# A graph attention kernel: the two gathers of a step of layer 1 stand apart, with the matmul stages rearranged around them

## The chip, the cores and the metric

The kernel runs on one core of a Trainium2 chip. A core has five engines with an instruction stream each: TensorE (PE in the profile; its weight loads are PEld), VectorE (DVE), ScalarE (ACT), GpSimd (POOL) and SyncE (SP). They run side by side and wait for each other by semaphores only. DMA engines move data between DRAM and the core's memory; a DMA is issued by an instruction of some engine. The metric is the time of one execution on the device in microseconds (us), as the median of several runs.

## The reference: what is computed

```python
B, N, C = x.shape            # 8, 2048, 64
H, D, _ = Wh.shape           # 4, 64
mask = graph + jnp.eye(N, dtype=graph.dtype) > 0
h = jnp.einsum('bnc,hdc->bhnd', x, Wh)
out_h = _gat_layer(h, mask[None, None], bh[None, :, None, :])
cat = jnp.transpose(out_h, (0, 2, 1, 3)).reshape(B, N, H * D)
z = jax.nn.leaky_relu(cat, negative_slope=0.2)
h2 = jnp.einsum('bnk,dk->bnd', z, Wo)
out2 = _gat_layer(h2, mask[None], bo)
z2 = jax.nn.leaky_relu(out2, negative_slope=0.2)
mu = jnp.mean(z2, axis=-1, keepdims=True)
var = jnp.mean(jnp.square(z2 - mu), axis=-1, keepdims=True)
out = (z2 - mu) * jax.lax.rsqrt(var + LN_EPS) * gamma + beta
...
x = _layernorm(x + out, axis=-1)
```

`_gat_layer(h, mask, b)` takes scores h times h transposed, keeps those where the mask is set, applies softmax over the neighbours and sums the neighbours' h with these weights, plus b. So there are two layers of attention over a graph: the first with four heads per batch element, the second with one. The adjacency is sparse. Node 0 has the most neighbours, and the number falls with the node's index.

## The kernel before

The first 56 nodes ("hubs") have so many neighbours that they are treated densely, in a prologue. The other 1992 nodes are cut into 166 sets of 12. For a set, the kernel finds the union of its nodes' neighbours, at most 128 of them, and gathers their rows from a table in DRAM: row m holds the values of node m for all 8 batch elements, with columns of ones for the softmax sums. From these 128 rows the scores of the 12 nodes are computed as small dense blocks, with a mask.

Layer 1 runs in 83 groups of two sets. Its loop (L1110, `for i in range(-4, NG + 3)`) is a software pipeline written out by hand: a step i works on several groups, each at another stage. The order in which the stages are written is the order of the instructions on each engine, since every engine works through its stream in order. The framework adds the semaphore waits where one engine's result is another's input, or where a buffer is still in use. In step i, in the order before, stand:

- scores of group i + 1 (L826, 64 small matmuls) and weigh (L831, DVE: scores minus mask, out of the tensor memory);
- project of group i - 1 (L532, 16 matmuls with the head weights) and leaky (L519, ACT: bias);
- two ACT copies xTg (L1129) of the gathered rows that the step before transposed into bank 0 and bank 1;
- lift (L838, ACT: exp), values of group i (L851, 32 matmuls: weights times gathered rows), and invert (L858 reciprocal and L859 multiplication on DVE, which gives osb);
- the two gathers of group i + 5 (L797 on POOL, an indirect DMA each). Their buffers come from a ring of ten, so they wait until values of group i have read theirs;
- own_rows (L805, POOL: copies the sets' own columns of x, for four sets, in every second step), and from step 30 load_own (SP: loads of xb) and add_beta (L933, POOL: adds beta to a piece of x that layer 2 uses) in alternate steps;
- leak (L524, DVE: the leaky ReLU of z);
- side jobs: the rest of the hubs' layer 1 (`hub_later`: turn_back, through_heads, to_table, for two halves, in steps 0 to 5), adjacency loads, and the building of the neighbour lists of the sets of later groups (`make_keys`, `pick`);
- second_maps of group i - 2 (L885, 8 matmuls with Wo), second_rows of group i - 3 (L895, one transpose), columns of group i + 4 (L811, 4 matmuls: the sets' own rows times the Gram matrices of the heads);
- keep_own (L890 on DVE, then L891 on POOL), keep_rows (L899 on DVE, then L902, writes to layer 2's table by SP), keep_columns (L817, ACT);
- turn bank 0 (L513, 4 transposes of gathered rows), turn_values (L868, 4 transposes of osb) with keep_values (L875, two ACT copies), turn bank 1 (L513).

The tensor memory holds one buffer for each of the tags S (scores), C (`cat`: project, second_maps, second_rows and columns of a step share it by slices) and O (values and turned values), and the two banks. Layer 2 begins after the loop. In the names of the rows `g` is a tile of gathered rows, `y` the kept columns, `e` the weights, `o` the values, `own` and `rowt` the results on their way to layer 2.

Of the kernel before, what the change touches and what calls it, by code (L numbers as in the profile page):

```python
# [359 lines left out]
def fast_kernel(ctx: ExitStack, tc: tile.TileContext, x, adj, Wh, bh, Wo, bo, gamma, beta, out, flag):  # L360
# [262 lines left out]
    def hub_later(t, new):  # L623
# [13 lines left out]
        def through_heads():  # L637
            cat = new(f"cath{t}", "C")
            project(held.pop(("oth", t)), cat, n)
            z = held["zh", t] = leaky(cat, n, f"zh{t}")  # L640
            leak(z)
# [158 lines left out]
    def own_rows(m):  # L800

        w = min(4, NS - 4 * m)
        t = held["x", m] = work.tile([P, 2 * GM], F32, tag="xo", name=f"xo{m}", bufs=2)
        src = xT[:, :, HUB:].rearrange("c q (k s) -> c s q k", s=NS)[:, 4 * m:4 * m + w]
        nc.gpsimd.tensor_copy(t[:, :w * 48].rearrange("c (s q k) -> c s q k", s=w, q=Q), src)  # L805
# [195 lines left out]
    own_rows(0)  # L1001
    own_rows(1)
# [107 lines left out]
    for i in range(-4, NG + 3):  # L1110
# [4 lines left out]
        if i >= 1 and slow and len(slow) % 3:  # L1115
            slow.pop(0)()
        cat = one(f"cat{i}", "C") if i <= NG else None
        if i < NG:
            ph, pr = cat[:, 0, 384:384 + GM], cat[:GM, 1, 384:512]
        else:  # L1120
            cat = one(f"cat{i}", "S" if i == NG + 1 else "C")
            ph, pr = cat[:, 0, :GM], cat[:GM, 1, :P]
        if 0 <= i - 1 < NG:
            project(held.pop(("ot", i - 1)), cat, GM)
            held["z", i - 1] = leaky(cat, GM, f"z{i - 1}")
        if 0 <= i + 2 < NG:
            t = held["T", 1, i + 2] = work.tile([P, 2, 512], F32, tag="xTg", name=f"xTg{i + 2}", bufs=3)
            for k in range(2):
                nc.scalar.copy(t[:, k, :], bank[k])  # L1129
        if 0 <= i + 1 < NG:  # L1130
            lift(i + 1)
        if 0 <= i < NG:
            op = one(f"o{i}", "O")
            values(i, op)
            invert(i, op)
        if 0 <= i + LOOK < NG and i > -3:
            for j in range(2):
                gather(table1, 2 * (i + LOOK) + j, 1, rows_tile)
        if NG - LOOK <= i < NG - 1:
            for j in range(2):  # L1140
                k = 2 * (i - NG + LOOK) + j
                hub_block(k, rows_tile(f"gh{k}"))
        if i + 6 < NG and i % 2 == 0 and i >= -2:
            own_rows((i + 6) // 2)
        if i >= 60 and i % 2 == 0 and ahead_of_second:
            ahead_of_second.pop(0)()
        if 0 <= (i - 30) // 2 <= NV:
            (add_beta if i % 2 else load_own)((i - 30) // 2)
        if 0 <= i - 1 < NG:
# [325 lines left out]
```

## Time and profile before

| | us |
|---|---|
| time, median of 3 runs | 1018.35 |
| the runs | 1017.01, 1018.35, 1022.75 |
| profiled execution: span | 1021.0 |

The busy time of the engines in the whole span, its course in 40 slices, and the costliest groups that concern the loop of layer 1:

```profile
PE 807.8 (79%) x18437; PEld 685.5 (67%) x18437; DVE 617.2 (60%) x1376; ACT 521.4 (51%) x1042; POOL 481.3 (47%) x614
...
PE   3976679899999999999999998419786676667760
...
PEclk9989989999999999999999999658999999999985
```

```profile
L797 POOL DMA_INDIRECT g<-table,index x166 | 176.6, 1064 | 207.2 <-PE o L851 165.7
...
L826 PE MATMUL s<-y,xTg 64*64 64x48 f32 x5312 | 115.4, 222 | 5.4 <-issue 3.5
...
L851 PE MATMUL o<-g,e 128*64 128x65 f32 x2656 | 98.0, 226 | 2.4 <-issue 2.4
...
L811 PE MATMUL cat<-xo,gram 128*128 128x192 f32 (+1 forms) x320 | 65.0, 326 | 0.0
```

In the first block the share of the span stands in brackets and the number of instructions behind the x. A digit of the slices is the busy share in tenths (9 is 90% or more), one slice being 1021.0 / 40 = 25.5 us; PEclk is the granted clock of TensorE in tenths. Slices 7 to 24, about 157 to 620 us, are the loop of layer 1. In the second block a row is a group of instructions by line, engine and operands: number, busy time in us and mean of one in ns, then the idle time of the engine just before them and what ended most of it; "issue" is time in which the engine waited for nothing that the profile shows. Matmuls overlap, so that the mean of one is longer than the distance from one to the next. In rows of the timeline, further down, consecutive instructions of one kind are one row: start, length from the first one's start to the last one's end, number, and in brackets the idle time before it with what ended it.

### The profile page before, as it was taken

To read this page: it belongs to the slowest core of one execution; us is meant where nothing else is said; L and a number is where in the kernel's file an instruction comes from. 1 tells how busy PE (TensorE), PEld (TensorE's weight loads), DVE (VectorE), ACT (ScalarE), POOL (GpSimd) and SP (SyncE) were. 2 spreads that over 40 slices of the span, in tenths; PEclk is the share of its full clock that TensorE was granted. 3 is DMA by queue.
4 is the path that set the end of the run, shared out by engine and by line. 5 is a ranking of instruction groups with operands and counts; after the bars stand their busy time and mean duration, and the time that the engine had idled before them with its cause. 6 is when DMAs were issued, how large, how long until landed. Compare 5 with 4: busy or idle time off the path is not lost.

```text
span 1021.0 us, 42671 instructions
## 1 busy us (share of the span) xinstructions
PE 807.8 (79%) x18437; PEld 685.5 (67%) x18437; DVE 617.2 (60%) x1376; ACT 521.4 (51%) x1042; POOL 481.3 (47%) x614
## 2 busy tenths in 40 slices
PE   3976679899999999999999998419786676667760
PEld 2644457788898888888888887307665555555750
DVE  3449844678777777745555555002267766766795
ACT  2423335556566666666666665005445645555651
POOL 6533214474454555556556630750456556655100
PEclk9989989999999999999999999658999999999985
DMA  8876412453233344444444432764345555445221
GB/s 184 238 208 171 118 44 59 131 134 80 75 91 83 103 124 123 120 124 115 120 119 113 120 86 75 193 184 128 91 112 141 152 147 142 125 134 138 76 53 29
DMA packets 81790, 122.52 MB, mean 120 GB/s; under 512 B 35568, under 2 KB 51852, under 8 KB 81594
## 3 DMA queue, kind: packets, MB, share of 16 engines
q0 software_dynamic: 26784, 65.84, 24.9%
q1 hardware_dynamic: 37702, 49.57, 16.3%
q10 hardware_dynamic: 17108, 4.30, 2.3%
q8 instruction: 147, 2.41, 1.0%
q14 instruction: 49, 0.40, 0.1%
HBM read 123.91 MB, written 18.48 MB: 139 GB/s over the span
## 4 chain that ended last, share of the span: by engine, by line
PE 56%; DVE 13%; issue 9%; ACT 8%; another core or an unknown queue 6%; DMA 4%; POOL 2%; SPq 1%; DVEq 0%; POOLq 0%; ACTq 0%
PE s L826 10%; PE o L851 8%; PE bank L513 7%; PE t L513 6%; PE cat L811 5%; ACT xts L1368 3%; DMA raw<-in_adj_dram 3%; PE cat L532 3%; PE o L868 3%; PE cat L885 3%; PE bank L1234 2%; PE bank L1223 2%; PE cat L895 2%; PE o L1253 2%
## 5 line engine op out<-in xcount | busy, mean ns | idle before, releaser
L797 POOL DMA_INDIRECT g<-table,index x166 | 176.6, 1064 | 207.2 <-PE o L851 165.7
L797 POOL DMA_INDIRECT rows<-table,index x166 | 170.0, 1024 | 147.3 <-PE o L1253 87.5
L831 DVE TENSOR_TENSOR e<-s,mask 128x768 f32<-128x768 f32 x83 | 79.4, 957 | 95.2 <-PE s L826 94.8
L826 PE MATMUL s<-y,xTg 64*64 64x48 f32 x5312 | 115.4, 222 | 5.4 <-issue 3.5
L513 PE MATMUL t<-ident,rows 128*128 128x128 f32 x664 | 91.6, 280 | 31.8 <-issue 30.4
L826 PEld LDWEIGHTS s<-y,xTg 64*64 64x64 f32 x5312 | 98.9, 134 | 25.6 <-issue 20.2
L1368 ACT COPY xts<-t 128x1024 f32<-128x1024 f32 x83 | 79.9, 1011 | 56.2 <-PE t L513 48.5
L513 PEld LDWEIGHTS t<-ident,rows 128*128 128x128 f32 x664 | 76.3, 144 | 40.9 <-issue 39.8
L513 PE MATMUL bank<-ident,g 128*128 128x128 f32 x664 | 100.2, 274 | 0.2 <-ACT otbh L634 0.2
L851 PE MATMUL o<-g,e 128*64 128x65 f32 x2656 | 98.0, 226 | 2.4 <-issue 2.4
L519 ACT ACTIVATE z<-cat,bhp 128x192 f32<-128x192 f32 x166 | 60.7, 417 | 73.9 <-PE cat L532 70.8
L851 PEld LDWEIGHTS o<-g,e 128*64 128x64 f32 x2656 | 85.8, 138 | 12.8 <-issue 3.0
L1129 ACT COPY xTg<-bank 128x512 f32<-128x512 f32 x166 | 89.1, 596 | 0.5 <-PE bank L513 0.3
L1223 PE MATMUL bank<-xts,share 128*32 128x128 f32 x1328 | 56.2, 278 | 34.4 <-issue 19.7
L513 PEld LDWEIGHTS bank<-ident,g 128*128 128x128 f32 x664 | 79.9, 142 | 2.8 <-DVE keysi L766 0.6
L838 ACT ACTIVATE e<-e,shifts 128x768 f32<-128x768 f32 x83 | 80.0, 964 | 2.5 <-DVE e L831 2.5
L817 ACT COPY y<-cat 128x384 f32<-128x384 f32 (+1 forms) x80 | 40.7, 509 | 68.5 <-DVE rowt L899 37.3
L598 ACT ACTIVATE e<-e,shifts 128x896 f32<-128x896 f32 x32 | 33.4, 1043 | 81.4 <-DVE e L595 65.6
L1223 PEld LDWEIGHTS bank<-xts,share 128*32 128x32 f32 x1328 | 38.1, 109 | 50.9 <-issue 44.2
L681 POOL TENSOR_SCALAR a<-raw 120x1024 bf16<-120x1024 int32 (+1 forms) x34 | 38.5, 1135 | 62.1 <-DMA raw<-in_adj_dram 34.7
L811 PE MATMUL cat<-xo,gram 128*128 128x192 f32 (+1 forms) x320 | 65.0, 326 | 0.0
L858 DVE RECIPROCAL rall<-o 64x8 f32<-64x8 f32 x166 | 34.1, 205 | 50.5 <-PE o L851 49.1
(190 smaller groups left out, 1563.0 us busy)
## 6 DMA issues: line engine op xcount, KB each, us to landing
raw<-in_adj_dram SPq DMA_DIRECT2D x32, 480.0 KB
table<-xb SPq DMA_DIRECT2D x22, 256.0 KB
xr_s<-table SPq DMA_DIRECT2D x21, 256.0 KB
table<-x SPq DMA_DIRECT2D x16, 260.0 KB
x<-in_x_dram ACTq DMA_DIRECT2D x32, 128.0 KB
table<-rowt SPq DMA_DIRECT2D x164, 24.4 KB
xb<-in_x_dram SPq DMA_DIRECT2D x164, 24.0 KB
out_dram<-y_s SPq DMA_DIRECT2D x162, 24.0 KB
```

Source lines behind the costliest of these rows:

```text
L513: nc.tensor.transpose(tp[:, q * P:(q + 1) * P], rows[:, q, 1:1 + P], ident)
L519: nc.scalar.activation(z[:, hp], cat[:, :, hp * n:(hp + 1) * n], AF.Identity, bias=bhp[:, hp:hp + 1], scale=1.0)
L797: nc.gpsimd.indirect_dma_start(out=t.rearrange("n q c -> n (q c)"), out_offset=None, in_=table, in_offset=bass.IndirectOffsetOnAxis(ap=ind ...
L811: nc.tensor.matmul(cat[:, k, 2 * GM:2 * GM + n], gram[:, g % 2 * 2 + k, :], held["x", g // 2][:, :n], start=True, stop=True)
L817: nc.scalar.copy(held["y", g // 2][:, :n, g % 2 * 2:g % 2 * 2 + 2], cat[:, :, 2 * GM:2 * GM + n].rearrange("p a n -> p n a"))
L826: nc.tensor.matmul(sp[half(r), p, (q * 2 + j) * M:(q * 2 + j + 1) * M], xt[half(p), j, q, half(r)], y[half(p), (j * Q + q) * M:(j * Q + q ...
L831: nc.vector.tensor_tensor(e[:, :16 * M].rearrange("p (a q n) -> p a q n", a=2, q=Q), sp[:, :, :8 * M].rearrange("p a (q n) -> p a q n", q= ...
L838: nc.scalar.activation(e[:, :16 * M], e[:, :16 * M], AF.Exp, bias=shifts[:, 0:1], scale=1.0)
L851: nc.tensor.matmul(op[half(p), j, o0:o0 + K1], e[:, c0:c0 + 64], rw[j][:, q, sums(p)], start=True, stop=True)
L1129: nc.scalar.copy(t[:, k, :], bank[k])
L1223: nc.tensor.matmul(sp[q * 32:(q + 1) * 32, k, :], bd[u % 3][:, k, q, :], xt[:, s % 2, q, :], start=True, stop=True, tile_position=(0, q * 32))
L1368: nc.scalar.copy(t, tp)
```

## The change

The step's stages get a new order. On PE: scores, project, columns, second_rows, side jobs, values, second_maps, both turns (bank 0 and bank 1), turn_values. On ACT the xTg copies stand before leaky, and keep_columns comes before values. On DVE keep_rows follows weigh, and keep_own still follows leak. On POOL the first gather stands right behind values, then the copy of keep_own, then own_rows, now for two sets in every step and no longer for four in every second one, and then the second gather; add_beta comes last. The hubs' jobs are all called at one place, one a step from step 0, and the projected hub values use tag S for their buffer in the tensor memory, not C. `cat` is allocated in the same way in every step.

```diff
--- before.py
+++ after.py
@@ -635,7 +635,7 @@
                            pt.rearrange("c (w n) -> c w n", w=8)[:, :, :HV].rearrange("c w (n h) -> c h w n", h=H))
 
         def through_heads():
-            cat = new(f"cath{t}", "C")
+            cat = new(f"cath{t}", "S")
             project(held.pop(("oth", t)), cat, n)
             z = held["zh", t] = leaky(cat, n, f"zh{t}")
             leak(z)
@@ -797,12 +797,16 @@
         nc.gpsimd.indirect_dma_start(out=t.rearrange("n q c -> n (q c)"), out_offset=None, in_=table,
                                      in_offset=bass.IndirectOffsetOnAxis(ap=index[:, s:s + 1], axis=0), **bound)
 
-    def own_rows(m):
-
-        w = min(4, NS - 4 * m)
-        t = held["x", m] = work.tile([P, 2 * GM], F32, tag="xo", name=f"xo{m}", bufs=2)
-        src = xT[:, :, HUB:].rearrange("c q (k s) -> c s q k", s=NS)[:, 4 * m:4 * m + w]
-        nc.gpsimd.tensor_copy(t[:, :w * 48].rearrange("c (s q k) -> c s q k", s=w, q=Q), src)
+    def own_rows(m, j):
+
+        w = min(2, NS - 4 * m - 2 * j)
+        if j == 0:
+            held["x", m] = work.tile([P, 2 * GM], F32, tag="xo", name=f"xo{m}", bufs=2)
+        if w <= 0:
+            return
+        s0 = 4 * m + 2 * j
+        src = xT[:, :, HUB:].rearrange("c q (k s) -> c s q k", s=NS)[:, s0:s0 + w]
+        nc.gpsimd.tensor_copy(held["x", m][:, j * 96:j * 96 + w * 48].rearrange("c (s q k) -> c s q k", s=w, q=Q), src)
 
     def columns(g, cat):
 
@@ -998,8 +1002,9 @@
     for g in range(LOOK - 2):
         for j in range(2):
             gather(table1, 2 * g + j, 1, rows_tile)
-    own_rows(0)
-    own_rows(1)
+    for m in range(2):
+        for j in range(2):
+            own_rows(m, j)
     for t in range(2):
         hub_end(t)
     for e in es:
@@ -1112,46 +1117,29 @@
             sp = one(f"s{i + 1}", "S")
             scores(i + 1, sp)
             weigh(i + 1, sp)
-        if i >= 1 and slow and len(slow) % 3:
-            slow.pop(0)()
-        cat = one(f"cat{i}", "C") if i <= NG else None
-        if i < NG:
-            ph, pr = cat[:, 0, 384:384 + GM], cat[:GM, 1, 384:512]
-        else:
-            cat = one(f"cat{i}", "S" if i == NG + 1 else "C")
-            ph, pr = cat[:, 0, :GM], cat[:GM, 1, :P]
+        cat = one(f"cat{i}", "S" if i == NG + 1 else "C")
+        ph, pr = cat[:, 0, 384:384 + GM], cat[:GM, 1, 384:512]
         if 0 <= i - 1 < NG:
             project(held.pop(("ot", i - 1)), cat, GM)
-            held["z", i - 1] = leaky(cat, GM, f"z{i - 1}")
         if 0 <= i + 2 < NG:
             t = held["T", 1, i + 2] = work.tile([P, 2, 512], F32, tag="xTg", name=f"xTg{i + 2}", bufs=3)
             for k in range(2):
                 nc.scalar.copy(t[:, k, :], bank[k])
+        if 0 <= i - 1 < NG:
+            held["z", i - 1] = leaky(cat, GM, f"z{i - 1}")
+        if 0 <= i + 4 < NG + NG % 2:
+            columns(i + 4, cat)
+        if 0 <= i - 3 < NG:
+            second_rows(i - 3, pr)
+            keep_rows(i - 3, pr)
         if 0 <= i + 1 < NG:
             lift(i + 1)
-        if 0 <= i < NG:
-            op = one(f"o{i}", "O")
-            values(i, op)
-            invert(i, op)
-        if 0 <= i + LOOK < NG and i > -3:
-            for j in range(2):
-                gather(table1, 2 * (i + LOOK) + j, 1, rows_tile)
-        if NG - LOOK <= i < NG - 1:
-            for j in range(2):
-                k = 2 * (i - NG + LOOK) + j
-                hub_block(k, rows_tile(f"gh{k}"))
-        if i + 6 < NG and i % 2 == 0 and i >= -2:
-            own_rows((i + 6) // 2)
-        if i >= 60 and i % 2 == 0 and ahead_of_second:
-            ahead_of_second.pop(0)()
-        if 0 <= (i - 30) // 2 <= NV:
-            (add_beta if i % 2 else load_own)((i - 30) // 2)
-        if 0 <= i - 1 < NG:
-            leak(held["z", i - 1])
+        if 0 <= i + 4 < NG + NG % 2:
+            keep_columns(i + 4, cat)
         if i >= 0:
             if turns():
                 some(1)
-            if slow and len(slow) % 3 == 0:
+            if slow:
                 slow.pop(0)()
             more(1)
             if todo3 and i == todo3[0][0]:
@@ -1162,29 +1150,39 @@
                 picks = pick(2)
                 done = NS
             assert i + 1 + LOOK >= NG or 2 * (i + 1 + LOOK) + 1 < ready
-
+        if 0 <= i < NG:
+            op = one(f"o{i}", "O")
+            values(i, op)
+            invert(i, op)
+        if 0 <= i - 1 < NG:
+            leak(held["z", i - 1])
+        if 0 <= i + LOOK < NG and i > -3:
+            gather(table1, 2 * (i + LOOK), 1, rows_tile)
+        if NG - LOOK <= i < NG - 1:
+            for j in range(2):
+                k = 2 * (i - NG + LOOK) + j
+                hub_block(k, rows_tile(f"gh{k}"))
         if 0 <= i - 2 < NG:
             second_maps(i - 2, ph)
-        if 0 <= i - 3 < NG:
-            second_rows(i - 3, pr)
-        if 0 <= i + 4 < NG + NG % 2:
-            columns(i + 4, cat)
+        if 0 <= i + 3 < NG:
+            for j in range(2):
+                turn(bank[j], rows[1, 2 * (i + 3) + j])
+        if 0 <= i < NG:
+            turn_values(i, op)
+            keep_values(i, op)
         if 0 <= i - 2 < NG:
             keep_own(i - 2, ph)
-        if 0 <= i - 3 < NG:
-            keep_rows(i - 3, pr)
+        if i >= -2 and 2 * ((i + 6) // 2) < NG:
+            own_rows((i + 6) // 2, i % 2)
+        if 0 <= i + LOOK < NG and i > -3:
+            gather(table1, 2 * (i + LOOK) + 1, 1, rows_tile)
+        if i >= 60 and i % 2 == 0 and ahead_of_second:
+            ahead_of_second.pop(0)()
+        if 0 <= (i - 30) // 2 <= NV:
+            (add_beta if i % 2 else load_own)((i - 30) // 2)
         for _ in range((2 if i < 22 or i % 2 else 1) if i >= 0 else 0):
             if not turns():
                 some(1)
-        if 0 <= i + 4 < NG + NG % 2:
-            keep_columns(i + 4, cat)
-        if 0 <= i + 3 < NG:
-            turn(bank[0], rows[1, 2 * (i + 3)])
-        if 0 <= i < NG:
-            turn_values(i, op)
-            keep_values(i, op)
-        if 0 <= i + 3 < NG:
-            turn(bank[1], rows[1, 2 * (i + 3) + 1])
         if NG - 3 <= i < NG:
             hub_step(i - NG + 3, bank[0])
     for k in range(3, 9):
```

## The prediction

> **What bounds the kernel now.** I read the windows view first, over the loop of layer 1 (columns: length, busy time with instruction count of PE, PEld, DVE, ACT and POOL, granted clock, DMA share, GB/s), cut at the starts of the scores stage of steps 6, 24, 31, 78 and 79.
>
> ```profile
> 210.22:313.10 102.88, 99.41 (x2488) 87.71 (x2487) 85.66 (x224) 63.26 (x145) 52.15 (x71) 1.00 0.35 90
> 351.19:609.85 258.66, 252.41 (x6441) 226.02 (x6440) 160.88 (x401) 168.29 (x381) 150.18 (x186) 1.00 0.43 117
> 609.85:614.66 4.81, 4.81 (x139) 4.35 (x138) 2.89 (x7) 3.31 (x9) 0.27 (x1) 1.00 0.30 71
> ```
>
> From step 6 on PE is busy 97% of the time at full granted clock; DVE and ACT have a third free and POOL 40% and more. So PE's order sets the pace. The first two windows hold 18 and 47 steps: 5.72 and 5.50 us each. The last row is a step in which no gather of this loop is issued any more: 4.81 us. Its PE rows in the timeline (start, length, work):
>
> ```profile
> 609.85 1.15 PE L826 MATMUL s<-y,xTg 64*64 64x48 f32 x64
> 610.82 0.53 PE L532 MATMUL cat<-otb,whT 64*64 64x96 f32 x16
> 611.28 1.15 PE L851 MATMUL o<-g,e 128*64 128x65 f32 x32
> 612.26 0.50 PE L885 MATMUL cat<-z,woT 128*64 128x96 f32 x8
> 612.69 0.32 PE L895 MATMUL cat<-ident,own 128*96 128x128 f32 x1
> 612.85 0.58 PE L811 MATMUL cat<-xo,gram 128*128 128x96 f32 x4
> 613.26 0.60 PE L513 MATMUL bank<-ident,g 128*128 128x128 f32 x4
> ```
>
> From start to start: scores 0.97, project 0.46, values 0.98, second_maps 0.43, second_rows 0.16, columns 0.41. Columns are half as wide here; full ones take 0.65 (403.80 to 404.45 below), a turn 0.44 (404.45 to 404.89). So 4.81 + 0.24 = 5.05 us is a step of PE alone, and 0.4 to 0.45 us of a 5.50 step is something else. An ordinary step, first its PE rows, then those of DVE, POOL and ACT:
>
> ```profile
> 403.22 0.50 PE L885 MATMUL cat<-z,woT 128*64 128x96 f32 x8
> 403.65 0.31 PE L895 MATMUL cat<-ident,own 128*96 128x128 f32 x1
> 403.80 0.82 PE L811 MATMUL cat<-xo,gram 128*128 128x192 f32 x4
> 404.45 0.60 PE L513 MATMUL bank<-ident,g 128*128 128x128 f32 x4
> 404.89 0.55 PE L868 MATMUL o<-ident,osb 112*128 112x112 f32 x4
> 405.27 0.60 PE L513 MATMUL bank<-ident,g 128*128 128x128 f32 x4
> 405.81 0.56 PE L826 MATMUL s<-y,xTg 64*64 64x48 f32 x24
> 406.62 0.87 PE L826 MATMUL s<-y,xTg 64*64 64x48 f32 x40 [0.25 <-issue]
> ```
>
> ```profile
> 403.43 0.42 DVE L858 RECIPROCAL rall<-o 64x8 f32<-64x8 f32 x2 [0.53 <-PE o L851]
> 403.89 0.69 DVE L859 TENSOR_TENSOR osb<-o,rall 128x512 f32<-128x512 f32 x1
> 404.50 0.55 DVE L524 SCALAR_TENSOR_TENSOR z<-z 128x384 f32<-128x384 f32 x1
> 405.22 0.26 DVE L890 COPY own<-cat 128x96 f32<-128x96 f32 x1 [0.17 <-PE cat L811]
> ```
>
> ```profile
> 403.56 1.02 POOL L797 DMA_INDIRECT g<-table,index  x1 [2.25 <-PE o L851]
> 404.88 1.05 POOL L797 DMA_INDIRECT g<-table,index  x1 [0.31 <-DMA table<-rowt]
> 405.95 1.27 POOL L933 TENSOR_TENSOR xb<-xb,bet 128x512 f32<-128x512 f32 x1
> ```
>
> ```profile
> 406.73 0.54 ACT L875 COPY otb<-o 128x192 f32<-128x192 f32 x2 [0.44 <-PE o L868]
> ```
>
> After the second gather has begun (404.88) PE starts 4 + 4 + 24 = 32 matmuls and then stands still inside the scores, put down to "issue", until 406.62: 0.69 us after that gather's end at 405.93. ACT's copy L875 gets the signal of a transpose whose row ended at 405.44 only at 406.73. I read it so: while a gather's instruction runs on POOL, and about half a microsecond longer, PE's completions can come late, and PE can run only some 32 matmuls ahead. Slow matmuls (columns, turns: 0.10 to 0.16 us each) spend that allowance slowly, so the first gather costs nothing; fast ones (scores 0.015, project and values 0.03) spend it at once. Over 29 steps the waits view gives
>
> ```profile
> PEld s L826 <- issue: 9.0, 43, 0.5
> ...
> PE s L826 <- issue: 1.9, 9, 0.4
> ```
>
> which is 10.9 / 29 = 0.37 us a step. That is what the change can win or multiply.
>
> **The change, part by part.** Counts of matmuls, ACT and DVE work stay; own_rows (L805) is cut in halves. Let X be the moment at which the values' last signal arrives (403.41 above) and s the start of the next scores.
>
> *First gather.* It still starts at X + 0.15 and lies over second_maps, eight turns and L868, all slow or few: 20 matmuls, no loss.
>
> *L868.* The turns ahead of it are now second_maps and both L513 stages: 0.43 + 0.44 + 0.44, from X - 0.19, so PE is at L868 at X + 1.12. Its input osb ends with L859 at 404.58 = X + 1.17. So PE waits about 0.1 us that it did not wait, taken as 0.13 with the signal; the bounds are 0 (before, the four columns and a turn covered it) and 0.69, the length of L859, if DVE comes to it so late. Then s = X + 1.77.
>
> *Second gather.* On POOL it now stands behind keep_own's copy L891, which waits for DVE's L890, and behind half of own_rows. DVE runs L858, L859, L524 to 405.05 (X + 1.64), then L890 0.26; the POOL costs are
>
> ```profile
> L891 POOL COPY own<-own 128x96 f32<-128x96 f32 x59 | 16.1, 273 | 14.4 <-DVE own L890 14.3
> L805 POOL COPY xo<-xT 128x192 f32<-128x192 f32 (+1 forms) x28 | 14.4, 515 | 0.2
> ```
>
> and a gather starts 0.15 after what it waited for (403.56 after X). So 1.64 + 0.26 + 0.27 + 0.26 + 0.15 = X + 2.58, that is s + 0.8. It ends at s + 1.85, and the stretch with late completions at about s + 2.35. In that stretch PE now has: 10 scores left, 16 of project, 4 columns, 1 second_rows = 31 matmuls, which last until s + 0.97 + 0.46 + 0.65 + 0.16 = s + 2.24. With an allowance of 32 the loss is 0.1 us instead of 0.37.
>
> *What waits on it.* add_beta (L933, 1.27 us) now follows the second gather: X + 2.58 + 1.03 + 1.27 = X + 4.9, ahead of the next first gather at X + 5.3. The rows of a gather are used five groups later. SP's writes from keep_rows come earlier and nothing waits for them. On DVE keep_rows now stands between weigh and invert: if the scores' signal too comes only at s + 2.35, weigh (0.96) and keep_rows (0.28) end at s + 3.6, and the values' signal is there at s + 5.25 - 1.77 = s + 3.5: L859, and with it L868, up to 0.15 later. I charge half of that in the 47 steps from 31 on, in most of which xb is loaded, and nothing before.
>
> *Steps 0 to 5.* The hub jobs run here. PE waited
>
> ```profile
> PE hh L650 <- DVE e L831: 2.1, 2, 1.1
> PE cat L532 <- ACT zh L519: 1.8, 2, 0.9
> ```
>
> 3.9 us in all. The jobs now come behind columns and second_rows, when weigh is nearly done, and through_heads no longer takes the tile that project needs. I take all 3.9; the bounds are 0 (the waits return at L851) and twice the sum, 8.
>
> The span of the profiled execution is on the page:
>
> ```profile
> span 1021.0 us, 42671 instructions
> ```
>
> *Sum.* Per step -0.37 + 0.13 + 0.10 = -0.14 in the 25 steps 6 to 30, so -3.5; -0.14 + 0.07 in 47 steps, so -3.3; hub -3.9: together -10.7. The profiled span, 1021.0, lies 2.65 above the median 1018.35 and inside the runs shown (1017.01 to 1022.75); off the median the sum is 1007.6, and I say **1007**. Below: all of the 0.45 goes, on 72 steps, with 0.13 for L868: -23, and hub -8: 987. Above: the case A.
>
> **The rivals.** A, slower: the allowance is already half spent when the gather begins, because fast matmuls are under way and unfinished. One step before shows just this, its second gather 0.88 after the scores' start:
>
> ```profile
> 444.85 1.15 PE L826 MATMUL s<-y,xTg 64*64 64x48 f32 x64
> 445.73 1.02 POOL L797 DMA_INDIRECT g<-table,index  x1 [2.09 <-issue]
> 445.82 0.91 PE L532 MATMUL cat<-otb,whT 64*64 64x96 f32 x14
> ...
> 447.25 0.96 DVE L831 TENSOR_TENSOR e<-s,mask 128x768 f32<-128x768 f32 x1 [2.79 <-PE s L826]
> 447.38 1.15 PE L851 MATMUL o<-g,e 128*64 128x65 f32 x32
> ```
>
> PE stops after 14 of project's 16, before the slow columns could help, and values start 2.53 after the scores' start instead of 1.43: 1.1 us lost. The changed step has its gather there every time. Then a step costs -0.37 + 0.13 + 1.1 = +0.86: 72 steps +62, hub -4, 1076; if only steps 31 to 77, which carry the xb loads as this one does, lose so, +40 - 3.5 - 4 = 1051. It decides when fewer than some 26 matmuls fit after the gather's start: 10 + 16, the door to the columns. The Trainium skill speaks for A: in "TensorE: Matmul & The Clock Gate", Part 3, The mechanism, PE has a reorder window 64 deep. Taken as 32 pairs of weight load and matmul that agrees with the 32 counted at 404.88; and a window counts from the oldest unfinished pair, which would leave less than 32 here.
>
> Against A: where L885's signal is late because of the first gather (until 404.58 + 0.5 = X + 1.67), L890 and the second gather move up to 0.2 us back, further onto the columns. And it is one step, in which SP's loads of xb ran beside the gather; how much of the allowance is spent in a quieter step no row shows.
>
> C, a draw: PE gets two or three columns far, stops at about s + 1.9 and loses 0.3 to 0.36; a step costs +0.06 to +0.12, 72 of them +4 to +9, less the hub's 3.9: 1019 to 1023, I say 1020.
>
> D, slower a little: the place of a gather does not matter, so the change does not do what it moves things for; the pause of 0.37 stays and L868's 0.13 comes on top: 72 x 0.13 - 3.9 = +5.5, 1024. Against it: the gather-free step, and that pauses end with gathers. The Trainium skill says as much as D in "SBUF — State Buffer", Who interferes with whom: "PE and ACT never wait on anyone." The rows at 406.62 and 406.73 speak against it here.
>
> **How the numbers follow.** The forecast 0.45, its own range 987 to 1013; A 0.30; C 0.18; D 0.07. About 0.5%, 5 us, is what a measurement of this kernel tells from no change, so same is 1013 to 1023. D lies just beyond; half of it counts as same, as does C: faster 0.45, same 0.21, slower 0.34. The range goes from 987 to 1062: below it perhaps 0.04, above it the dearer half of A, 0.15.
>
> **What would show it.** In the changed profile the second gather should start 0.7 to 1.0 after the scores' start, over project and columns. Right: the scores take 1.15 in a row, columns start about 1.45 after them, weigh waits little, a step takes about 5.25 and the "issue" idle time of PE falls. Wrong towards A: project is cut with idle "issue", weigh waits over 2 us, values start 2.9 or more after the scores, steps take 6. L868 should wait about 0.1 for osb; if it waits 0.3 or more, keep_rows behind a late weigh does it. Steps 0 to 5 should lose the waits of L650 and L532. A second gather that starts after s + 1.1 would put the pause into values and make my sum too small by some 0.2 a step.

## The result, and the profile after

The changed kernel takes 1203.31 us (median of 4 runs, 1197.25 to 1213.59), the kernel before 1020.55 beside it: a measured ratio of 1.1812 (95% interval 1.1742 to 1.1883; the two medians by themselves give 1.179). It is 18% slower, outside the predicted range. In a second measurement (c_after below) the ratio was 1.1793 (1.1718 to 1.1868). In the changed kernel's line numbers L830 is the scores, L815 columns, L899 second_rows, L855 values, L889 second_maps, L872 turn_values, L809 own_rows; runs with more lines ahead of a stage have it a few lines lower.

The page of the changed kernel, cut to what answers to the lines shown of before:

```profile
span 1195.4 us, 42594 instructions
...
PE 879.1 (74%) x18437; PEld 721.6 (60%) x18437; DVE 618.6 (52%) x1376; ACT 533.0 (45%) x1042; POOL 482.7 (40%) x655
...
PE 56%; issue 14%; ACT 13%; DVE 11%; DMA 3%; POOL 2%; another core or an unknown queue 1%; SPq 0%; POOLq 0%; ACTq 0%; DVEq 0%
...
L815 PE MATMUL cat<-xo,gram 128*128 128x192 f32 (+1 forms) x320 | 75.1, 359 | 87.7 <-ACT z L519 72.9
```

The group of columns had 0.0 us of idle time before it in the kernel before. Now PE stands 87.7 us ahead of it, most of it ended by `z`, which is leaky on ACT. ACT has 13% of the chain that ended last; it had 8% before.

Windows by steps, of the changed kernel (columns as in the prediction: length, busy time and number of PE, PEld, DVE, ACT, POOL, granted clock, DMA share, GB/s): steps 0 to 5, 6 to 23 and 31 to 77 as the prediction counts them. That count is one below the loop's index i: the windows hold i = 1 to 6, 7 to 24 and 32 to 78. From here on steps are called by i.

```profile
169.27:227.25 57.98, 40.89 (x868) 34.01 (x867) 28.57 (x76) 23.77 (x53) 20.95 (x29) 0.85 0.32 87
227.25:374.17 146.92, 118.45 (x2488) 96.74 (x2488) 84.88 (x223) 66.01 (x144) 54.19 (x82) 0.92 0.25 66
...
426.47:783.55 357.08, 296.35 (x6441) 248.65 (x6441) 162.54 (x403) 174.03 (x378) 150.81 (x209) 0.95 0.31 85
```

The first of these windows in the kernel before, which the prediction did not quote:

```profile
165.38:210.22 44.84, 37.28 (x867) 31.93 (x866) 27.20 (x72) 22.63 (x52) 23.06 (x31) 0.96 0.43 114
```

The three stretches are 13.1, 44.0 and 98.4 us longer, 155.6 of the 174.4 by which the span grew. In the last one a step takes 357.08 / 47 = 7.60 instead of 5.50, with the same 6441 matmuls. An ordinary step of the changed kernel, i = 46, its PE rows, then leaky on ACT and the second gather on POOL:

```profile
534.51 1.15 PE L830 MATMUL s<-y,xTg 64*64 64x48 f32 x64
535.48 0.79 PE L532 MATMUL cat<-otb,whT 64*64 64x96 f32 x13
536.68 0.39 PE L532 MATMUL cat<-otb,whT 64*64 64x96 f32 x3 [0.41 <-issue]
537.99 0.89 PE L815 MATMUL cat<-xo,gram 128*128 128x192 f32 x4 [0.91 <-ACT z L519]
...
537.11 0.73 ACT L519 ACTIVATE z<-cat,bhp 128x192 f32<-128x192 f32 x2 [0.93 <-PE cat L532]
...
535.40 1.03 POOL L797 DMA_INDIRECT g<-table,index  x1 [0.22 <-issue]
```

The second gather starts 0.89 us after the scores. PE stops in project after 13 of its 16 matmuls; project ends at 537.07, 2.56 after the scores' start instead of 1.50. Only then can ACT begin leaky (537.11 to 537.84), and only after leaky do columns start, at 537.99. So two stops follow each other, 1.06 and 0.91 us. Two of the steps i = 31 to 77, 49 and 75, have the gather well after project, and in them the first stop is gone and the second is not. At i = 75, with the scores' start at 754.17:

```profile
755.14 0.53 PE L532 MATMUL cat<-otb,whT 64*64 64x96 f32 x16
756.53 0.92 PE L815 MATMUL cat<-xo,gram 128*128 128x192 f32 x4 [0.86 <-ACT z L519]
...
755.97 1.02 POOL L797 DMA_INDIRECT g<-table,index  x1 [0.16 <-issue]
```

It takes 6.26 us (the next scores start at 760.43), the ordinary one 7.35; i = 49 takes 6.73.

A third case stands between them. At i = 43 the scores start at 511.43 and the gather 1.19 later:

```profile
512.40 0.53 PE L532 MATMUL cat<-otb,whT 64*64 64x96 f32 x16
514.87 0.92 PE L815 MATMUL cat<-xo,gram 128*128 128x192 f32 x4 [1.94 <-ACT z L519]
...
514.08 0.73 ACT L519 ACTIVATE z<-cat,bhp 128x192 f32<-128x192 f32 x2 [0.98 <-PE cat L532]
...
512.62 1.02 POOL L797 DMA_INDIRECT g<-table,index  x1 [0.15 <-issue]
```

Project is not cut and ends at 512.93, while the gather runs. Yet ACT waits for project's signal until 514.08, 0.44 after the gather's end at 513.64, columns wait for leaky 1.94, and the step takes 7.34 like an ordinary one. So it is not PE's stop by itself that makes the step long: beside a gather the signal of PE's finished work comes late, and in this order everything behind leaky is late with it.

### The profile page after: what moved, and what is told of

The parts are those of the page before. It is cut to its first block, busy times and chain, and to the rows that moved or that the text cites. A ratio compares the mean times of both kernels' runs of the same rounds, so it can differ in the third digit from the quotient of the medians.

```text
span 1195.4 us, 42594 instructions
## 1 busy us (share of the span) xinstructions
PE 879.1 (74%) x18437; PEld 721.6 (60%) x18437; DVE 618.6 (52%) x1376; ACT 533.0 (45%) x1042; POOL 482.7 (40%) x655
## 4 chain that ended last, share of the span: by engine, by line
PE 56%; issue 14%; ACT 13%; DVE 11%; DMA 3%; POOL 2%; another core or an unknown queue 1%; SPq 0%; POOLq 0%; ACTq 0%; DVEq 0%
PE o L855 8%; PE bank L513 7%; PE s L830 7%; PE cat L815 6%; PE cat L532 5%; ACT z L519 5%; PE t L513 5%; ACT xts L1366 3%; PE cat L889 3%; PE o L872 3%; DMA x<-in_x_dram 2%; PE oh L609 1%; PE bank L1232 1%; DVE var L1299 1%; PE sh L591 1%
## 5 line engine op out<-in xcount | busy, mean ns | idle before, releaser
L797 POOL DMA_INDIRECT g<-table,index x166 | 170.3, 1026 | 286.6 <-PE o L855 251.0
L815 PE MATMUL cat<-xo,gram 128*128 128x192 f32 (+1 forms) x320 | 75.1, 359 | 87.7 <-ACT z L519 72.9
L879 ACT COPY otb<-o 128x192 f32<-128x192 f32 x166 | 44.9, 322 | 211.3 <-PE o L872 207.6
L815 PEld LDWEIGHTS cat<-xo,gram 128*128 128x128 f32 x320 | 51.6, 195 | 102.0 <-ACT z L519 44.2
L855 PEld LDWEIGHTS o<-g,e 128*64 128x64 f32 x2656 | 97.2, 155 | 20.9 <-issue 19.8
L855 PE MATMUL o<-g,e 128*64 128x65 f32 x2656 | 109.7, 244 | 0.0
L830 PE MATMUL s<-y,xTg 64*64 64x48 f32 x5312 | 103.1, 221 | 7.8 <-issue 7.6
L830 PEld LDWEIGHTS s<-y,xTg 64*64 64x64 f32 x5312 | 89.9, 134 | 22.5 <-issue 11.0
L532 PE MATMUL cat<-otb,whT 64*64 64x96 f32 x1328 | 78.4, 252 | 19.5 <-issue 18.1
L903 DVE TENSOR_TENSOR rowt<-cat,bob 96x128 f32<-96x128 f32 x83 | 24.0, 289 | 120.4 <-PE cat L899 98.5
L681 POOL TENSOR_SCALAR a<-raw 120x1024 bf16<-120x1024 int32 (+1 forms) x34 | 37.9, 1118 | 103.6 <-DMA raw<-in_adj_dram 75.8
```

The lines of the kernel that those rows point to most:

```text
L532: nc.tensor.matmul(cat[half(j), s, hp * n:(hp + 1) * n], whT[half(s), h * D:(h + 1) * D], ot[half(s), h, :], start=True, stop=True)
L797: nc.gpsimd.indirect_dma_start(out=t.rearrange("n q c -> n (q c)"), out_offset=None, in_=table, in_offset=bass.IndirectOffsetOnAxis(ap=ind ...
L815: nc.tensor.matmul(cat[:, k, 2 * GM:2 * GM + n], gram[:, g % 2 * 2 + k, :], held["x", g // 2][:, :n], start=True, stop=True)
L830: nc.tensor.matmul(sp[half(r), p, (q * 2 + j) * M:(q * 2 + j + 1) * M], xt[half(p), j, q, half(r)], y[half(p), (j * Q + q) * M:(j * Q + q ...
L855: nc.tensor.matmul(op[half(p), j, o0:o0 + K1], e[:, c0:c0 + 64], rw[j][:, q, sums(p)], start=True, stop=True)
```

## The experiments

Three theories stood against each other. T: two costs add up, the second gather over project (1.1 us a step) and columns waiting for leaky (0.9). W: the wait for leaky is everything. G: the gather's place is everything.

Columns need nothing of leaky's; they write columns 192 to 383 of the tile `cat`, and leaky reads columns 0 to 191. But both lie in one tile, and so in the same two banks of the tensor memory, and the wait covers more than the columns read. In the Trainium skill, "PSUM — Partial Sum Buffer", section PSUM bank collisions raise a hardware error, the rule is to guard this memory by bank and not by address; the rows above and the run e5 below agree with it. Whether the wait is kept by bank or by tile they do not tell apart, since e5 leaves both.

The runs fell on chips of two kinds: on one the kernel before takes 1018 us, as for the prediction, on the other 889. Every ratio is to the kernel before on the same chip.

| run | before | ratio (95% interval) | step, mean of i = 31 to 77 |
|---|---|---|---|
| c_before, the kernel before | 1018 | one run | 5.49 |
| c_after, the changed kernel | 1018 | 1.179 (1.172 to 1.187) | 7.57 |
| e5, columns in banks | 1018 | 1.092 (1.085 to 1.098) | 6.36 |
| e6, side jobs back | 1018 | 1.184 (1.176 to 1.191) | 7.63 |
| e1, columns in banks | 889 | 1.061 (1.051 to 1.070) | 5.53 |
| e2 and e16, gathers together | 889 | 1.131 (1.122 to 1.140) and 1.132 (1.128 to 1.136) | 6.33 and 6.33 |
| e3 and e11, both | 889 | 1.061 (1.051 to 1.070) and 1.064 (1.054 to 1.074) | 5.44 and 5.44 |
| e4, columns back | 889 | 1.032 (1.024 to 1.040) | 5.55 |
| e7, own_rows two steps ahead | 889 | 1.044 (1.038 to 1.050) | 5.43 |
| e8 and e14, gather held back | 889 | 1.051 (1.046 to 1.056) and 1.044 (1.035 to 1.054) | 5.42 and 5.42 |
| e9, ACT's order | 889 | 1.062 (1.057 to 1.067) | 5.84 |
| e10, e13, e15, before with the gather late | 889 | 1.017 (1.011 to 1.023), 1.015 (1.006 to 1.024), 1.012 (1.006 to 1.018) | 5.35, 5.29 and 5.32 |
| e12, before with both gathers timed | 889 | 1.011 (1.007 to 1.015) | 5.28 |

**Columns in other banks (e1, e5).** The two banks of the turned rows are free between the xTg copies and the next turns:

```diff
-            nc.tensor.matmul(cat[:, k, 2 * GM:2 * GM + n], gram[:, g % 2 * 2 + k, :], ...
+            nc.tensor.matmul(bank[k][:, :n], gram[:, g % 2 * 2 + k, :], ...
...
-        ph, pr = cat[:, 0, 384:384 + GM], cat[:GM, 1, 384:512]
+        ph, pr = cat[:, 0, 384:384 + GM], bank[1][:GM, 384:512] if i < NG - 3 else cat[:GM, 1, 384:512]
```

keep_columns is two copies. In e1 (and e3) second_rows uses bank 1 in the last steps too and there writes over part of the hubs' sums of layer 2; the amount of work is the same.

> The changed kernel, but columns and second_rows write into bank 0 and bank 1 and no longer into the two banks that leaky reads, and keep_columns is two copies; order and gathers as changed. Theory T (two costs that add: the second gather over project, about 1.1 us a step, and columns waiting for leaky, about 0.9): the wait for leaky goes, the stop in project stays, a step takes 5.05 + 0.13 + 1.1 = 6.3 us, the time is about 1070 and columns start at 2.6 after the scores. Rival W (the wait for leaky is all of it, the stop in project only ends where PE would wait anyway): a step takes 5.3, the time is about 1005. Rival G (the gather is all of it): no change, 1200.

> The kernel before, unchanged, for a profile on the same chip as the three others. The four runs so far were on a chip on which the kernel before takes 890 and not 1018. If that is because PE's completions are held up less by the gathers there, its steps 31 to 77 are near the 5.05 of PE alone (5.05 to 5.2) with scores of 1.15 in a row, and the gathers of layer 2 cost PE less; if the gathers do not matter, steps stay at 5.5 and the difference lies elsewhere.

> The changed kernel, unchanged, on the same chip. Theory T (stop in project by the second gather, 1.1, plus columns waiting for leaky, 0.9): on a chip like the first 7.35 a step and a ratio of 1.18; on the other one, where the two gathers together left no stop, only the wait for leaky: 6.3 to 6.6 a step and a ratio of 1.13. Theory W (the wait alone): 7.35 on both.

> The changed kernel with columns and second_rows (but for its last six steps) in bank 0 and bank 1. Theory T: the wait of columns for leaky is gone (columns start 1.45 after the scores on the quick chip, 2.6 on the first); a step takes 6.3 on a chip like the first (ratio 1.05 to 1.06 with the early steps' loss), 5.4 to 5.55 on the other. Theory W: 5.3 on both.

On a chip of 1018 (e5) a step falls from 7.57 to 6.36, so W is out and so is G: there are two costs. The fall of 1.21 is more than the wait: ten steps of c_after with a lower clock (see the next section) are gone with it, and without them c_after's mean is 7.23. Two of e5's steps, i = 52 and 49, PE and the second gather on POOL; in the second step the gather does not run until 512.11:

```profile
527.30 1.15 PE L831 MATMUL s<-y,xTg 64*64 64x48 f32 x64
528.27 0.85 PE L532 MATMUL cat<-otb,whT 64*64 64x96 f32 x14
529.51 0.32 PE L532 MATMUL cat<-otb,whT 64*64 64x96 f32 x2 [0.39 <-issue]
529.76 0.92 PE L815 MATMUL bank<-xo,gram 128*128 128x192 f32 x4
...
528.20 1.02 POOL L797 DMA_INDIRECT g<-table,index  x1 [0.23 <-issue]
```

```profile
508.65 1.15 PE L831 MATMUL s<-y,xTg 64*64 64x48 f32 x64
509.62 0.53 PE L532 MATMUL cat<-otb,whT 64*64 64x96 f32 x16
510.08 0.92 PE L815 MATMUL bank<-xo,gram 128*128 128x192 f32 x4
...
512.11 1.04 POOL L797 DMA_INDIRECT g<-table,index  x1 [2.79 <-PE o L856]
```

Columns now follow project at once in both. With the gather at 0.90 they start 2.46 after the scores, without it 1.43. That step takes 5.32 (the next scores start at 513.97), the other 6.36: the gather costs 1.04 us. i = 75, with the gather at 1.80, takes 5.32 too. At i = 43 and 64 the gather starts at 1.19; there project is not cut and columns start at 1.42, and the step still takes 6.03 and 6.04.

On a chip of 889 the same order with the gather at the same place (e1) has no stop; in a step whose scores start at 500.11, project and columns on PE, leaky and the gather:

```profile
501.08 0.56 PE L532 MATMUL cat<-otb,whT 64*64 64x96 f32 x16
501.57 0.92 PE L815 MATMUL bank<-xo,gram 128*128 128x192 f32 x4
...
501.82 0.73 ACT L519 ACTIVATE z<-cat,bhp 128x192 f32<-128x192 f32 x2
...
500.91 1.02 POOL L797 DMA_INDIRECT g<-table,index  x1 [0.22 <-issue]
```

Here PE issues all 16 of project during the gather, and ACT has their signal by 501.82, before the gather's end at 501.93; in the ordinary step above it came at 537.11, 0.68 after the gather's end. So what a gather costs PE differs between chips. The step was as expected on both kinds of chip (5.53 and 6.36). The ratio of 1.05 to 1.06 expected of e5 was not met (1.092): its steps i = 0 to 23 take 185.0 us, those of c_before 145.2.

**Gathers together (e2, e3, e11, e16).** The second gather directly behind the first, in the changed kernel (e2, e16) and with columns in banks (e3, e11):

```diff
             gather(table1, 2 * (i + LOOK), 1, rows_tile)
+            gather(table1, 2 * (i + LOOK) + 1, 1, rows_tile)
...
-        if 0 <= i + LOOK < NG and i > -3:
-            gather(table1, 2 * (i + LOOK) + 1, 1, rows_tile)
```

> The changed kernel with the second gather directly behind the first, all else as changed. Theory T: the second gather then lies over L872 and the scores as before the change and loses 0.37; the wait for leaky stays with 0.9; a step takes 5.05 + 0.13 + 0.37 + 0.9 = 6.45, the time is about 1085. Rival W (the wait is all of it): no change, 1200. Rival G (the gather's place is all of it): a step of 5.5, 1018.

> The changed kernel with both edits: columns and second_rows in bank 0 and bank 1, the second gather directly behind the first. Theory T: both costs go, a step takes 5.05 + 0.13 + 0.37 = 5.55 and the time is 1015 to 1025, that of the kernel before. If a third thing in the new order costs time, it stays above 1030.

> The changed kernel with columns and second_rows in bank 0 and bank 1 and the second gather directly behind the first. On a chip on which the kernel before takes 1018, theory T gives 5.32 (the step of this order with no stop, seen in steps 49 and 75 of the run with columns in banks) plus the old stop of 0.15 to 0.4 in the scores: 5.5 to 5.7 a step against 6.36 with the gathers apart. Rival (the stop does not come from the gather): 6.3 to 6.4. On a chip of 889 both give 5.32.

> The changed kernel with only the second gather moved, directly behind the first. On a chip of 1018, theory T: the stop in project (1.07 a step) gives way to the old one in the scores (0.15 to 0.4), the wait of columns for leaky stays: 6.4 to 6.7 a step against 7.37, ratio 1.10 to 1.12. Rival W (the stop in project only stands where PE would wait for leaky anyway): 7.2 to 7.4, ratio 1.17 to 1.18. On a chip of 889: 6.3 and 1.13 as before.

All four fell on chips of 889, so the numbers in e2's and e3's expectations, made for 1018, do not apply. They measure the wait for leaky by itself: 6.33 against 5.44, 0.89 us a step. e2's waits of PE in steps 31 to 77 (total, times, longest) agree:

```profile
PE cat L815 <- ACT z L519: 42.3, 46, 1.7
```

That is 0.92 each. They cannot tell whether the gather's cost goes when the gather is moved on a chip of 1018; e16 repeats e2, on a chip of 889 again. That it does rests on the steps with a late gather in the changed kernel and in e5; no run moves the gather on such a chip.

**The gather elsewhere (e4, e8, e10, e13, e14, e15).** e4 puts columns, second_rows, keep_rows and keep_columns back behind second_maps. e10, e13 and e15 are the kernel before with only this:

```diff
-            for j in range(2):
-                gather(table1, 2 * (i + LOOK) + j, 1, rows_tile)
+            gather(table1, 2 * (i + LOOK), 1, rows_tile)
...
             keep_own(i - 2, ph)
+            fill(i - 2, 3)
+        if 0 <= i + LOOK < NG and i > -3:
+            gather(table1, 2 * (i + LOOK) + 1, 1, rows_tile)
```

with add_beta behind it; `fill` repeats keep_own's copy on POOL. e8 and e14 are e7 (below) with three such copies instead of one.

> The changed kernel with columns, second_rows, keep_rows and keep_columns back behind second_maps, gathers apart as changed. Columns then come long after leaky, so no wait for it; the second gather starts some 0.2 us after the scores' start and PE stops inside the scores until about 0.5 after its end. Theory T: the stop costs 1.1 to 1.2, a step takes 6.25, the time is about 1065. Rival W: 5.2 to 5.5 a step, 1000 to 1018.

> The kernel before, its order on PE unchanged, with only the second gather moved on POOL: behind keep_own's copy (and three repeats of it), add_beta behind the gather; it so starts about 0.9 after the scores' start, over project, as in the changed kernel. Theory T: the stop in project costs 1.1 in place of 0.37: 6.1 to 6.3 a step and a ratio of 1.05 to 1.06 on a chip like the first. Rival W (only the wait for leaky made the change slow): 5.5 a step, ratio 1.00 to 1.01.

> The kernel before with only the second gather moved behind keep_own's copy and three repeats of it, add_beta behind the gather (a kernel that ran on a chip of 889, where it took 1.017 of before). On a chip of 1018 theory T: the gather starts about 0.9 after the scores, PE stops in project, 6.1 to 6.3 a step, ratio 1.04 to 1.06. Rival W (only the wait of columns for leaky made the change slow): 5.4 to 5.5 a step, ratio at most 1.02.

> The kernel before with only the second gather moved on POOL, behind keep_own's copy and three repeats of it, add_beta behind the gather. On a chip of 1018, theory T: the gather starts about 0.9 after the scores, PE stops in project, 6.0 to 6.3 a step, ratio 1.035 to 1.06. Rival W (only the wait of columns for leaky made the change slow): 5.4 to 5.5 a step, ratio at most 1.02. On a chip of 889: 1.015 as before.

> As the run above, with keep_own's copy repeated three times instead of once ahead of the second gather, which so starts some 0.5 us later, at 1.35 after the scores' start, when project is all but issued. Theory T: PE no longer stops in project; columns start at 1.45 to 1.7 after the scores; what is left is ACT's lateness (leaky and keep_columns only after the gather's end + 0.5): 5.5 to 6.0 a step on a chip like the first, about 1040 to 1060. Rival (a gather anywhere over the fast stages costs the same 1.1): 6.3 to 6.4 a step as before.

> The changed kernel with columns and second_rows in banks, own_rows two steps ahead, and three repeats of keep_own's copy ahead of the second gather (a kernel that ran on a chip of 889). On a chip of 1018 theory T: the gather starts 1.35 after the scores, project is nearly issued, columns start at 1.45 to 1.7; 5.5 to 6.0 a step with leaky and keep_columns late on ACT, against 6.36 with the gather at 0.88. Rival (a gather anywhere over fast stages costs 1.1): 6.3 to 6.4.

All of them met chips of 889, and there the gather did not land where it was meant to: in the median of the steps it starts 1.65, 2.02 and 1.81 us after the scores in e10, e13 and e15 (0.9 was meant), 1.87 in e8 and e14 (1.35), 1.12 in e4 (0.2). On these chips its place moves a step by little: 5.43 with 1.22 (e7) against 5.42 with 1.87 (e8, e14); the gather late in the order before costs 1.2 to 1.7% of the whole. e4 gives 5.55, far from the 6.25 expected for 1018. These runs support only that without a long hold the gather's place does not matter much; they neither confirm nor refute T on a chip of 1018.

**The early steps (e6, e7).** The steps i = 4, 6, 8 and 10 of the changed kernel take 11.8 to 15.0 us. The waits of PE on columns and of POOL on load_adj over 169.27 to 264.82 (i = 1 to 10), and POOL's and PE's rows at i = 6:

```profile
PE cat L815 <- POOL xo L809: 14.9, 3, 7.0
...
POOL a L681 <- DMA raw<-in_adj_dram: 42.6, 7, 10.3
```

```profile
217.89 1.08 POOL L681 TENSOR_SCALAR a<-raw 120x1024 bf16<-120x1024 int32 x1 [6.29 <-DMA raw<-in_adj_dram]
...
220.40 0.33 POOL L809 COPY xo<-xT 128x96 f32<-128x96 f32 x1
...
220.78 1.65 PE L815 MATMUL cat<-xo,gram 128*128 128x192 f32 x4 [7.05 <-POOL xo L809]
```

POOL works in order: it waits for the adjacency (L681), then come the gather and keep_own's copy, and only then own_rows, whose half columns need now. Before, own_rows made both halves two steps ahead; now the second half comes at the end of an odd step, just before its use in the even one.

e6 moves only the block of side jobs back behind values, leak and the first gather. e7 takes e5 and makes own_rows for four sets again, two steps ahead, behind the second gather:

```diff
-        if i >= -2 and 2 * ((i + 6) // 2) < NG:
-            own_rows((i + 6) // 2, i % 2)
+        if 0 <= i - 2 < NG:
+            fill(i - 2, 1)
...
+        if i % 2 == 0 and i >= -2 and i + 6 < NG:
+            for j in range(2):
+                own_rows((i + 6) // 2, j)
```

> The changed kernel with the block of side jobs (hub jobs, adjacency loads on POOL, building of lists) back behind values, leak and the first gather. If their place ahead of values costs the early steps (steps 3 to 9 take 7 to 15 us after the change, 5 to 10 before), steps 0 to 23 lose 10 to 25 us of it and steps 24 to 77 stay as in the changed kernel; if the early steps only suffer from the wait for leaky like the others, nothing changes by more than 5 us.

> The changed kernel with columns and second_rows in bank 0 and bank 1 as in the run before, and own_rows again for four sets in every second step, two steps ahead, behind the second gather; in its old place POOL repeats keep_own's copy once, so that the second gather keeps its place. Theory O (in the early steps columns wait for own_rows, which POOL reaches only behind load_adj's wait for its DMA): steps 6 to 23 fall from 135 to 110 to 120 us, the waits of columns for xo are gone, steps 31 to 77 stay at 6.36; about 1085 on a chip like the first. Rival: the early steps wait for the gathers' rows or for the adjacency itself: no change beyond 5 us.

e6 changed nothing (i = 0 to 23 took 207.9 us, 203.9 in c_after): POOL's load_adj still stands ahead of own_rows. e7, on a chip of 889, is compared with e11 there, which differs from it also in the second gather's place. Steps i = 0 to 5 and 6 to 23 of e11, then of e7:

```profile
159.63:208.15 48.52, 37.45 (x846) 30.91 (x845) 25.95 (x69) 24.25 (x56) 18.39 (x26) 0.93 0.29 77
208.15:335.87 127.72, 105.74 (x2488) 88.46 (x2487) 83.86 (x224) 69.53 (x162) 55.33 (x84) 0.92 0.31 81
```

```profile
155.72:199.90 44.18, 37.51 (x846) 31.37 (x845) 25.72 (x69) 23.57 (x55) 17.27 (x25) 0.94 0.30 81
199.90:315.43 115.53, 102.39 (x2488) 85.87 (x2487) 83.50 (x224) 70.21 (x162) 62.47 (x105) 0.97 0.35 92
```

It gains 16.5 us; against e1, which has the gathers apart too, it gains 11.9 (171.6 to 159.7). PE's wait for `xo` up to 259 us is 6.0 in e7, and up to 262 us it was 20.9 in e11. So the lead of own_rows is a third cost. It does not account for all of the early loss: the order before takes 147.8 there on such a chip (e13).

**Two tries for a faster order (e9, e12).** e9 is e8 with keep_columns ahead of leaky and the xTg copies behind the turns. e12 is the kernel before, the second gather of a group held to the next step until leaky has ended, the first one after it, so that both lie over values' end and the slow stages.

```diff
+        if 0 <= i - 1 + LOOK < NG and i - 1 > -3:
+            if 0 <= i - 1 < NG:
+                nc.gpsimd.tensor_copy(gate, held["z", i - 1][:, 0, 0, :1])
+            gather(table1, 2 * (i - 1 + LOOK) + 1, 1, rows_tile)
         if 0 <= i + LOOK < NG and i > -3:
-            for j in range(2):
-                gather(table1, 2 * (i + LOOK) + j, 1, rows_tile)
+            gather(table1, 2 * (i + LOOK), 1, rows_tile)
```

> As the run above, and on ACT keep_columns ahead of leaky, the xTg copies right behind the turns. If ACT's order is what is left after the gather is held back, the step falls to 5.2 to 5.4 and the time to 1000 to 1020, about or a little below the kernel before; if not, it stays at 5.5 to 6.0.

> The kernel before, with its gathers moved on POOL so that neither ends over the scores or project: the second gather of the group before waits (through a copy of one column of z) for leaky and starts about 2.3 after the scores' start, the first gather follows at about 3.6. They then lie over values' end, second_maps, columns and turns, up to 4.7 + 0.5 after the scores' start. Theory T: the stop of 0.37 goes, a step takes 5.05 to 5.2, ratio 0.975 to 0.985 on a chip of 1018, 1.00 on one of 889. Rival: the stop moves into values and costs 0.3 or more there: ratio 1.00 to 1.02.

Both met 889 and neither beats the kernel before there. e9 is worse than e8 (5.84 against 5.42): second_maps writes `cat` and so waits for the now later leaky, 19.0 us in i = 31 to 77, the same trap again. e12's loop has an even step of 5.05 in the median, but the whole is 1.1% slower than before; where it loses that, no run shows. On a chip of 1018 neither was tried.

## Why the prediction was wrong

What bounds the kernel was read rightly: PE's order. In the changed kernel the first gather costs nothing, as forecast. The second starts 0.89 after the scores where 0.8 was worked out, and add_beta is out of the way in time. The signs named for A came: project is cut, and weigh waits 2.30 us in the ordinary step.

**The step that failed first** is the one on PE's order that took columns to follow project at once ("10 scores left, 16 of project, 4 columns, 1 second_rows = 31 matmuls, which last until ... s + 2.24"). Columns cannot follow at once: leaky reads the tile that they write. No part of the prediction named that wait, neither the list of what waits nor a rival, and it alone is 0.89 to 0.92 us a step, 43.1 us in the 47 steps of the last window:

```profile
PE cat L815 <- ACT z L519: 43.1, 47, 2.0
PE cat L532 <- issue: 13.0, 35, 0.4
```

The hint lay in the trace of before: L890, which reads what second_maps wrote, is put down as released by columns (`405.22 ... [0.17 <-PE cat L811]`), another slice of the same tile.

**Second, the allowance.** The forecast took 32 matmuls from the gather's start and a loss of 0.1; rival A took what the step at 444.85 showed, 1.1. The runs on chips of 1018 showed A: PE stops after 13 or 14 of project, 1.04 to 1.06 lost. Its chance was 0.30 and its price for all steps 1076. The nearest row deserved to be the forecast, and the count of 32, from a gather that began over slow turns, was carried to a gather that begins over fast scores. The Trainium skill's window of 64 entries ("TensorE: Matmul & The Clock Gate", Part 3, The mechanism), which A drew on, does not decide it: on the chips of 889 the same 16 matmuls pass. Nor is the count of matmuls the whole cost, as A had it too: at i = 43 of the changed kernel all 16 pass and the step is as long, because leaky gets PE's signal late. The 0.37 that was to be won adds idle times of matmuls and of weight loads, which overlap; the difference of steps, 5.50 less 5.05, is 0.45.

**Third, the early steps.** The hub jobs were to give 3.9 us back; the first window (i = 1 to 6) became 13.1 longer. A large part of that is own_rows' lost lead over columns, a wait of 14.9 us in i = 1 to 10. The prediction called its halving a mere cut and did not ask how many steps lie between the copy and its use.

**Fourth, the clock.** Ten of the 47 steps i = 31 to 77 take 8.75 to 8.86 us, against 7.35 for the ordinary one; their granted clock is 0.81 and that of the other 37 is 1.00. The mean is 7.57 with them and 7.24 without. Three windows of 2 us in such a step, i = 41:

```profile
497.25:499.25 2.00, 0.91 (x7) 0.74 (x8) 0.96 (x1) 1.21 (x3) 0.00 (x0) 1.00 0.51 128
499.25:501.25 2.00, 2.00 (x32) 1.76 (x32) 0.29 (x1) 0.97 (x2) 0.00 (x0) 0.61 0.03 8
501.25:503.25 2.00, 2.00 (x23) 1.78 (x20) 1.45 (x4) 0.00 (x0) 1.00 (x1) 0.54 0.12 29
```

After the stops, with PE busy 0.91 of 2.00 us, the granted clock is 0.61 and 0.54 in the next two windows. In e5, without the wait for leaky, it is 1.00 over i = 31 to 77. The Trainium skill, "TensorE: Matmul & The Clock Gate", What's actually happening, describes a gate set by how busy PE has been, with half rate after an idle window of about 3.4 us. The trace differs in that: no idle time of such a length stands here, only the two stops of about 1 us in every step, and the clock falls in about one step out of five. The forecast kept 1.00 since it saw no stops.

L868's wait for osb (L872 now), charged with 0.13, is 0.3 us in all 47 steps together: next to none. The order without any stop takes 5.32 a step (e5, at 508.65) where 5.05 + 0.13 was worked out: the other stages are 0.14 longer. Together, for an ordinary step: 5.32 + 1.06 + 0.91 = 7.29, measured 7.35. D's idea, that the place of a gather does not matter, holds nearly on the chips of 889 and fails on those of 1018. The sentence of the Trainium skill that D leans on ("SBUF — State Buffer", Who interferes with whom) is about ports of that memory and does not speak of signals.

## What to carry to other kernels

Before a matmul stage is moved forward, ask for each tile and bank it writes which engine still reads any part of it: disjoint slices of `cat` were one thing to the waits, and a wait that the old order hid for free becomes a stop in every step. When one odd step in the trace already shows the new arrangement, its price comes before a count taken from another situation. A copy that is cut in halves and spread over two steps may also lose its lead over its user; count the steps between.

## What the runs showed of the hardware

The same kernel takes 1018 us on some chips and 889 on others. Little of that lies in layer 1's steps i = 31 to 77 (5.49 in c_before, 5.29 in e13). Most lies in layer 2, whose code e13 shares with the kernel before: from i = 78 to the end c_before takes 412.7 us and e13 308.8. A stretch of layer 2 in c_before, and PE's wait there on its own issue ahead of one group of matmuls (total, times, longest):

```profile
650.00:980.00 330.00, 223.89 (x4880) 188.66 (x4876) 181.47 (x323) 164.56 (x288) 163.43 (x158) 0.91 0.48 133
```

```profile
PE bank L1223 <- issue: 19.7, 35, 1.9
```

The same in e13 on a chip of 889, where line numbers are 8 higher in this part:

```profile
600.00:865.00 265.00, 226.73 (x5464) 203.70 (x5466) 198.15 (x366) 181.22 (x326) 184.74 (x190) 0.98 0.63 181
```

```profile
PE bank L1231 <- issue: 0.6, 1, 0.6
```

PE gets through 4880 / 330 = 14.8 matmuls a us on the one and 5464 / 265 = 20.6 on the other; the group of L1223 has 19.7 us of stops without a releaser ahead of it in the first and 0.6 in the second. In the changed kernel's loop such stops stand beside gathers. On a chip of 1018 (i = 43 above) project's matmuls end at 512.93, the gather at 513.64, and ACT gets project's signal at 514.08; on one of 889 (e1) ACT has it by 501.82, before the gather's end at 501.93. That layer 2's stops come from its gathers too is likely, but was not tried. So a schedule tuned around this on one chip is not tuned on the other: the wait for leaky costs the same 0.9 us on both, the gather's place 1.04 us on the one and about 0.1 on the other (5.53 in e1 against 5.44 in e3). Why the chips differ, and whether it is the chip or a state that it was in, no run here shows.
